# Attention scores of a kernel's last stage: 64-row products with a masked second copy of the keys in place of 32-row products

## The chip, the cores and the metric

The kernel runs on one core of a Trainium2 chip. The metric is the device time of one execution in microseconds (us). TensorE (PE) multiplies matrices into PSUM, VectorE (DVE) and ScalarE (ACT) read PSUM and do element work, GpSimd (POOL) issues indirect transfers and sets memory, and SyncE (SP) issues most of the other transfers. All five run their own instruction streams and wait for each other through semaphores.

## The reference

Eight blocks follow each other over 8 x 256 tokens of 128 features, each as `x = layernorm(x + block(x))`: a recurrent scan, a dense mixture of experts, a latent attention, a second mixture of experts, a gated linear attention, a routed mixture of 160 experts, six layers of linear attention, and last `_L3_ffn_ref`, which is the one that is changed here:

```python
def _L3_ffn_ref(x, router_prob, norm_w, norm_b, q_w, q_b, k_w, k_b, v_w, v_b, o_w, o_b):
    B, T, D, E, H = (4, 256, 128, 4, 8)
    ...
    for e in range(e_cnt):                       # four segments of 64 tokens
        xn = _layernorm(x[:, e * n:(e + 1) * n, :], norm_w, norm_b)
        m = d // 2 ** e                          # 128, 64, 32, 16 features
        xm = xn[..., :m]
        qs.append(jnp.einsum('bnm,dm->bnd', xm, q_w[:, :m]) + q_b)
        ks_.append(jnp.einsum('bnm,dm->bnd', xm, k_w[:, :m]) + k_b)
        vs.append(jnp.einsum('bnm,dm->bnd', xm, v_w[:, :m]) + v_b)
    ...
    attn = jnp.einsum('bhqd,bhkd->bhqk', q, k) * scale      # 8 heads of 16 features
    attn = jax.nn.softmax(attn, axis=-1)
    attn_out = jnp.einsum('bhqk,bhkd->bhqd', attn, v)
    ...
```

So there are 8 heads of 16 features, and the scores of a head are a product over 16 features for 256 queries and 256 keys of each batch element. All data are float32.

## The kernel before

The 2048 tokens are kept as four groups g of 512 tokens (two batch elements of 256 each). Groups 0 and 1 are `first`, groups 2 and 3 are `second`. The two halves go through the blocks shifted against each other, so that a transfer-bound block of one half lies beside a compute-bound block of the other. A scheduler orders each engine's instructions when the kernel is built, by its own estimate of when each would be ready; on the chip every engine runs its stream strictly in that order, so an instruction that waits holds up what stands behind it. Pools give tiles their place in SBUF; a tile that lands where an older one lay waits for the older one's last user.

The routed experts (`place`, `routed_experts`, `gather`) of a half work like this: `place` on GpSimd scatters the tokens' rows to DRAM with 64 indirect transfers (L622), with small memsets (L541) between them as pauses; `routed_experts` loads blocks of rows (`xb<-placed`, L702) and of weights on SP's queue, transposes them (L136, tile ps_m) and multiplies (L729, L740); `gather` reads the results back with 64 indirect transfers (L751) that L757 sums up on DVE. `plan(second)` needs the end of the gated linear attention (L1044 to L1070), the router (L845) and counts (L553 to L560) of the second half, and starts GpSimd's second scatter.

The last part of the program is, in order: the six layers of linear attention of the first half (`layers`, L1110 to L1180; started beside the second half's routed experts), the last block of the first half (`l3_ffn`, whose `run` begins at L1227) beside the six layers of the second half, and the last block of the second half alone.

`l3_ffn` loads its weights on SP's queue (L63, L69, L1222), and GpSimd sets its value tiles (`vs`, L1214), its row maxima (`mx`, L1216) and `ob` (L1220). Then for each group: the tokens are normalized and transposed (L1244, L1246); queries and keys are made by L1254 for the head sets r = 0 and 1 and copied out of PSUM by ACT with a bias (L1255). A head set has four heads, each on a strip of 32 partitions: 16 features, one row that carries the row's maximum, and zeros. So q and k are [128 partitions, r, 512 tokens]. The scores of four heads are four products over 32 rows each, at partitions 0, 32, 64 and 96, into four PSUM banks. TensorE takes such a product as two records in the profile.

`maxima(b, i)` multiplies 128 queries with all 256 keys (L1280, two head sets in a bank) and DVE takes the maximum of every row (L1282). `shifted(b)` transposes the maxima and adds them to the queries' extra row (L1288), which meets the ones in the keys' extra row. `values(b, r)` multiplies 128 keys with all 256 queries (L1298, two key tiles in a bank), and ACT takes the exponentials (L1301). `summed` multiplies with the values (L1309), and `divided` transposes back and divides (L1319, L1321). The output product is L1357. The scores of a batch element are thus made twice, with 32 products of L1280 and 32 of L1298 for a group, so 128 of each in all. Score banks come from two PSUM pools of two banks each, which transposes and other products use as well.

Of the kernel before, what the change touches and what calls it, by code (L numbers as in the profile page):

```python
# [10 lines left out]
F32 = mybir.dt.float32  # L11
I32 = mybir.dt.int32
U32 = mybir.dt.uint32
AF = mybir.ActivationFunctionType
ALU = mybir.AluOpType
AX = mybir.AxisListType

P = 128
# [3 lines left out]
GT = NT // NG  # L22
# [20 lines left out]
def tile_post_ln_blocks(ctx: ExitStack, tc: tile.TileContext, I, out: bass.AP):  # L43
    nc = tc.nc
    V, S, G, PE = nc.vector, nc.scalar, nc.gpsimd, nc.tensor
# [8 lines left out]
    def bank(pool):  # L54
        return pool.tile([P, 512], F32, tag=pool.name, name=pool.name)

    def quarters(t):
        return t.rearrange("p (a b) -> p a b", b=P)

    def load(pool, key, tag=None, by=None):  # L60
        ap = I[key]
        t = pool.tile(list(ap.shape), F32, tag=tag or key, name=tag or key)
        (by or nc.sync).dma_start(out=t, in_=ap)  # L63
        return t
# [1138 lines left out]
    def l3_ffn(es):  # L1203
# [1 line left out]
        width = [D >> e for e in range(4)]  # L1205
        sc = D**-0.5
        wp = es.enter_context(tc.tile_pool(name="f3w", bufs=1))
        wq, wkk, wv, wo, nw, nb, qb, kb, first = (
            load(wp, "F3_" + k) for k in ("q", "k", "v", "o", "norm_w", "norm_b", "qb", "kb", "first")
        )  # L1210
        vb = load_row(wp, "F3_vb")
        for ln in lanes[:2]:
# [14 lines left out]
        def run(ln, g, banks):  # L1227
# [4 lines left out]
            def score():  # L1232
                turn[0] += 1
                return bank(banks[turn[0] % len(banks)])
# [3 lines left out]
            nT = wk.tile([P, GT], F32, tag="nT", name="nT")  # L1238
            nT = nT.rearrange("p (b e c) -> p b e c", b=2, e=4)
            pt = transpose4(zn, ln.ps).rearrange("p (b j) (s c) -> p b (j s) c", b=2, s=2)  # L1240
            for e in range(4):
                scale, bias = nw[:, e : e + 1], nb[:, e : e + 1]
# [4 lines left out]


            qk = wk.tile([P, 2, 2, GT], F32, tag="hT", name="qk")
            q, k = qk[:, 0], qk[:, 1]  # L1250
            for w, bias, t in ((wq, qb, q), (wkk, kb, k)):
                for r in range(2):
                    ps = score()
                    PE.matmul(ps, lhsT=w[:, r, :], rhs=nT.rearrange("p b e c -> p (b e c)"), start=True, stop=True)  # L1254
                    S.activation(t[:, r, :], ps, AF.Identity, bias=bias[:, r : r + 1])  # L1255
            pv = quarters(bank(ln.ps))
            for j in range(4):
                t = 2 * (j % 2)
                PE.matmul(
                    pv[:, j, :], lhsT=nT[:, j // 2, t : t + 2, :].rearrange("p e c -> p (e c)"), rhs=wv,  # L1260
                    start=True, stop=True,
# [6 lines left out]

            at = wk.tile([P, 4, D], F32, tag="qs", name="at")

            strips = [slice(32 * j, 32 * j + 32) for j in range(4)]
            oT = [None]

            def maxima(b, i):
                bs, c = slice(b * T, (b + 1) * T), b * T + i * P
                mx = ln.maxima[:, b]
                ps = [score().rearrange("p (r c) -> p r c", r=2) for _ in strips]
                for r in range(2):
                    for j, hp in enumerate(strips):
                        PE.matmul(ps[j][:, r, :], lhsT=q[hp, r, c : c + P], rhs=k[hp, r, bs], start=True, stop=True)  # L1280
                for j in range(4):
                    V.tensor_reduce(mx[:, i, :, j, DH], ps[j], AX.X, ALU.max, negate=True)  # L1282

# [7 lines left out]
            def values(b, r):  # L1291
                bs = slice(b * T, (b + 1) * T)
                exps = []
                ps = [score().rearrange("p (t c) -> p t c", t=2) for _ in strips]
                for t in range(2):
                    c = b * T + t * P
                    for j, hp in enumerate(strips):
                        PE.matmul(ps[j][:, t, :], lhsT=k[hp, r, c : c + P], rhs=q[hp, r, bs], start=True, stop=True)  # L1298
                for j in range(4):
                    ex = wk.tile([P, 2, T], F32, tag=("vs", "ks", "qT", "y2")[j], name="ex")  # L1300
                    S.activation(ex, ps[j], AF.Exp, scale=sc)  # L1301
                    exps.append(ex)
                return exps
# [11 lines left out]
            def divided(b):  # L1315
# [4 lines left out]
                for r in range(2):  # L1320
# [3 lines left out]
                    )  # L1324

            maxima(0, 0)
            maxima(0, 1)
            shifted(0)
            for r in range(2):
                exps = values(0, r)  # L1330
                maxima(1, r)
                summed(0, r, exps)
            divided(0)
            shifted(1)
            for r in range(2):
                summed(1, r, values(1, r))
# [29 lines left out]
    first, second = (0, 1), (2, 3)  # L1366
# [12 lines left out]
    with ExitStack() as moe:  # L1379
# [72 lines left out]
        gathers(second)  # L1452
    lanes += [Lane(tc, ctx, i) for i in (2, 3)]
    last = l3_ffn(ctx)
    run()
    for g in first:
# [6 lines left out]
def _layout(d):  # L1463

    a = {k: np.asarray(v) for k, v in d.items()}
    f = np.float32
    o = {"x": a["L0_attn_tokens"].reshape(NT, D)}
# [61 lines left out]
    w, d = a["L2_ffn_w_gate"].transpose(0, 2, 1), a["L2_ffn_w_down"].transpose(0, 2, 1)  # L1529
# [29 lines left out]
    def spread(w):  # L1559

        z = np.zeros(w.shape[:-1] + (2, 4, 32), w.dtype)
        z[..., :16] = w.reshape(w.shape[:-1] + (2, 4, 16))
        return z.reshape(w.shape[:-1] + (2, P))

    for k in "qk":
        o["F3_" + k] = spread(a[f"L3_ffn_{k}_w"].T)
        o[f"F3_{k}b"] = spread(a[f"L3_ffn_{k}_b"]).T.copy()
    o["F3_kb"][16::32] = 1.0
    o["F3_v"], o["F3_o"] = a["L3_ffn_v_w"].T, a["L3_ffn_o_w"].T
    o["F3_vb"], o["F3_ob"] = (a[f"L3_ffn_{k}_b"].reshape(1, D) for k in "vo")  # L1570
    o["F3_first"] = (lat[:, None] < (D >> np.arange(4))[None]).astype(f)
# [23 lines left out]
```

## Time and profile before

| what | us |
|---|---|
| median of 3 runs | 1978.19 (1975.71 to 1980.26) |
| profiled execution: its own time | 1984.49 |
| profiled execution: span from first to last instruction | 1982.6 |
| PE busy | 1726.8 (87%) |
| DVE busy | 1200.1 (61%) |
| ACT busy | 889.9 (45%) |
| POOL busy | 385.3 (19%) |
| mean granted TensorE clock | 0.919 |
| L1280, 128 products, records' busy time | 40.6 |
| L1298, 128 products, records' busy time | 44.9 |
| L1282, 64 maxima on DVE | 41.0 (0.682 each) |
| L1301, 64 exponentials on ACT | 34.9 (0.595 each at this shape) |

The profile is one execution. A line of its timeline gives the start in us, the duration, the engine, the line of the program, the operation, the tile written and those read, the shapes, and in brackets how long the engine idled before and what ended that wait. Matmuls of different strips overlap, so the busy time of TensorE is the time in which at least one is under way. A line of the windows view gives a stretch, its length, the busy time (and number of instructions) of PE, PEld (weight loads), DVE, ACT and POOL, then the granted TensorE clock as a share of full speed, the share of the DMA engines and GB/s. In the page's slices each digit is a fortieth of the span: the busy share, or the granted clock, in tenths.

### The profile page before, as it was taken

Reading aid. Unit: us, or ns where it says so; the run is one execution under the profiler, and the core shown is the slowest. Engines: PE = TensorE matmul, PEld = TensorE weight load, DVE = VectorE, ACT = ScalarE, POOL = GpSimd, SP = SyncE. Lnnn points to the kernel's source line nnn. Section 1 sums busy time; section 2 is a strip of 40 time slices with the busy share of each in tenths; the row PEclk is TensorE's granted clock in tenths of the full one; section 3 lists DMA queues with packets and bytes.
Section 4 is the critical chain, followed back from the end, with each engine's and each line's share of the span. In section 5 each row is a group of like instructions: output and inputs, shape, how many; then the busy total and the mean of one; then the engine's idle time right before and its main releaser. Section 6 shows DMA issues by size and latency. Waiting matters only on the chain. (4 is left out here: it accounts for less than half of the span.)

```text
span 1982.6 us, 38359 instructions
## 1 busy us (share of the span) xinstructions
PE 1726.8 (87%) x13996; PEld 1139.8 (57%) x13996; DVE 1200.1 (61%) x3912; ACT 889.9 (45%) x1992; POOL 385.3 (19%) x849
## 2 busy tenths in 40 slices
PE   8999889976999999999779674688877999998887
PEld 6888744544554446644467553466655776665554
DVE  4000255877878656799468811565677887575553
ACT  4555443824765345642424210244444665545433
POOL 1000000000000000007870587850287000000000
PEclk9999989978999999999789766899989999999887
DMA  3000079601434542336218765876011000000000
GB/s 101 3 4 3 3 208 276 178 10 50 116 101 109 157 131 76 102 103 181 58 42 252 249 211 183 262 243 192 22 40 37 1 1 1 1 6 6 1 1 11
DMA packets 161484, 184.97 MB, mean 93 GB/s; under 512 B 20336, under 2 KB 118640, under 8 KB 161296
## 3 DMA queue, kind: packets, MB, share of 16 engines
q1 hardware_dynamic: 143264, 149.47, 26.6%
q0 software_dynamic: 8192, 16.79, 2.9%
q10 hardware_dynamic: 9840, 16.26, 2.2%
q8 instruction: 111, 1.82, 0.4%
q14 instruction: 77, 0.63, 0.1%
HBM read 143.29 MB, written 56.16 MB: 101 GB/s over the span
## 5 line engine op out<-in xcount | busy, mean ns | idle before, releaser
L622 POOL DMA_INDIRECT placed<-x,pl x128 | 127.5, 996 | 990.2 <-DMA wu<-in_F_wu_dram 892.9
L434 ACT ACTIVATE h<-ps_m 128x512 f32<-128x512 f32 x196 | 116.0, 597 | 232.5 <-PE ps_m L432 210.7
L427 PE MATMUL ps_o<-h,wd 128*128 128x512 f32 x384 | 199.0, 603 | 6.4 <-DVE h L440 6.4
L432 PE MATMUL ps_m<-xT,wg 128*128 128x512 f32 x384 | 198.3, 599 | 3.8 <-ACT h L434 3.7
L360 PE MATMUL ps_s<-st,L_a 128*64 128x32 f32 x4096 | 193.2, 222 | 1.1
L360 PEld LDWEIGHTS ps_s<-st,L_a 128*64 128x64 f32 x4096 | 160.5, 136 | 30.0 <-ACT st L369 12.3
L440 DVE TENSOR_TENSOR h<-h,bc 128x512 f32<-128x512 f32 x192 | 131.2, 685 | 49.4 <-ACT h L434 41.9
L369 ACT ACTIVATE st<-ps_s 128x64 f32<-128x64 f32 x512 | 114.8, 224 | 102.3 <-PE ps_s L360 71.1
L751 POOL DMA_INDIRECT got<-made,pl x128 | 122.6, 958 | 135.1 <-DVE cx L1149 105.6
L437 PE MATMUL ps_m<-xT,wu 128*128 128x512 f32 x256 | 134.1, 606 | 6.2 <-ACT h L434 3.5
L541 POOL MEMSET idle<- 128x112 f32 (+1 forms) x576 | 124.8, 217 | 18.5
L427 PEld LDWEIGHTS ps_o<-h,wd 128*128 128x128 f32 x384 | 72.6, 193 | 96.0 <-issue 66.5
L740 PE MATMUL ps_o<-w,xg 64*64 64x128 f32 x1152 | 95.3, 315 | 32.0 <-DVE xg L735 16.4
L432 PEld LDWEIGHTS ps_m<-xT,wg 128*128 128x128 f32 x384 | 71.0, 191 | 86.0 <-issue 65.0
L438 DVE TENSOR_TENSOR h<-h,ps_m 128x512 f32<-128x512 f32 x132 | 89.8, 680 | 45.6 <-PE ps_m L437 40.0
L317 DVE SCALAR_TENSOR_TENSOR outsT<-xnT,L_skip,ps 128x64 f32<-128x64 f32 x32 | 10.4, 324 | 168.3 <-PE ps L305 168.3
L1169 PE MATMUL ps<-nT,A_w 128*128 128x512 f32 x192 | 97.7, 618 | 12.6 <-DVE hT L1171 7.8
L740 PEld LDWEIGHTS ps_o<-w,xg 64*64 64x64 f32 x1152 | 74.7, 155 | 49.2 <-DVE xg L735 20.7
L1175 PE MATMUL ps<-A_w,hT 128*128 128x128 f32 x768 | 98.6, 278 | 4.9 <-DVE hT L1171 3.9
L742 ACT COPY ob<-ps_o 128x512 f32<-128x512 f32 x72 | 42.1, 585 | 133.5 <-PE ps_o L740 99.2
L1175 PEld LDWEIGHTS ps<-A_w,hT 128*128 128x128 f32 x768 | 91.8, 192 | 12.7 <-DVE hT L1171 6.7
L729 PE MATMUL ps_m<-xg,w 128*64 128x64 f32 x1152 | 76.4, 257 | 24.8 <-DMA w<-in_F_w_dram 10.6
(370 smaller groups left out, 3496.7 us busy)
## 6 DMA issues: line engine op xcount, KB each, us to landing
bc<-comb SPq DMA_DIRECT2D x128, 256.0 KB
w<-in_F_w_dram SPq DMA_DIRECT2D x256, 96.0 KB
placed<-zero SPq DMA_DIRECT2D x72, 256.0 KB
xb<-placed SPq DMA_DIRECT2D x72, 256.0 KB
made<-ob ACTq DMA_DIRECT2D x72, 256.0 KB
w<-in_F_wg_dram SPq DMA_DIRECT2D x40, 256.0 KB
w<-in_F_wd_dram SPq DMA_DIRECT2D x40, 256.0 KB
bc<-comb SPq DMA_DIRECT2D x16, 512.0 KB
```

Of the source, the lines that this page charges most:

```text
L360: in_turn(PE.matmul(now[h][sides[c], n % HB // 2, n % 2, s].rearrange("p e f b -> p (e f b)"), lhsT=a_sb[:, n % 2, 4 * h + k, :], rhs=prev ...
L369: made_by = S.activation(st[:, t * 128 : t * 128 + 128].rearrange("p (k e z b) -> p k e z b", k=4, e=2, z=2)[:, :, :, 1], now[h][:, n % HB ...
L427: PE.matmul(acc[g], lhsT=w, rhs=h, start=begin, stop=end, skip_group_check=True)
L432: PE.matmul(pg, lhsT=wg, rhs=xT[g], start=True, stop=True)
L434: gate = S.activation(h, pg, func).ins
L437: PE.matmul(pu, lhsT=wu, rhs=xT[g], start=True, stop=True)
L440: V.tensor_tensor(h, h, bc[:, i * GT : (i + 1) * GT], ALU.mult)
L541: after, last = G.memset(idle[:, :columns], 0.0).ins, after
L622: i = G.indirect_dma_start(placed[h][:, :], bass.IndirectOffsetOnAxis(rw[:, j, c : c + 1], 0), x[g][:, j, :], None).ins
L740: PE.matmul(po[k, i // 2, :], lhsT=h[k, i // 2, :], rhs=wd[i], start=True, stop=True)
L751: i = G.indirect_dma_start(got[:, c, :], None, made[g // 2][:, :], bass.IndirectOffsetOnAxis(row[g][:, j, c : c + 1], 0)).ins
L1175: PE.matmul(po[:, j, :], lhsT=hT[:, f, j * P : (j + 1) * P], rhs=w2[:, f, :], start=(f == 0), stop=(f == 3),)
```

## The change

The keys are kept twice, as `k[0]` and `k[1]`. `k[0]` has the even strips' keys (heads 0 and 2 of a set) and zeros on the odd strips; `k[1]` has the odd strips' keys and zeros on the even ones. ACT makes the first with a scale of one or zero by partition (`strip[:, 0:1]`), and DVE makes the second from the same bank with `tensor_scalar`. A score product then runs over the 64 rows of a pair of strips, with the queries of both heads and the keys of one: the other head's rows add zeros. The products of strips 0 and 1 are on the upper 64 rows of the array, those of 2 and 3 on the lower 64, and the source asks for them in the order 0, 2, 1, 3. The number of products, their columns, their banks, the maxima and the exponentials stay. `k[1]` gets two tiles of 4 KB a partition in the stage's weight pool `wp`, the mask `F3_strip` is one more small load, and the bias of the keys `F3_kb` has two masked sets of columns.

```diff
--- before.py
+++ after.py
@@ -1205,8 +1205,8 @@
         width = [D >> e for e in range(4)]
         sc = D**-0.5
         wp = es.enter_context(tc.tile_pool(name="f3w", bufs=1))
-        wq, wkk, wv, wo, nw, nb, qb, kb, first = (
-            load(wp, "F3_" + k) for k in ("q", "k", "v", "o", "norm_w", "norm_b", "qb", "kb", "first")
+        wq, wkk, wv, wo, nw, nb, qb, kb, first, strip = (
+            load(wp, "F3_" + k) for k in ("q", "k", "v", "o", "norm_w", "norm_b", "qb", "kb", "first", "strip")
         )
         vb = load_row(wp, "F3_vb")
         for ln in lanes[:2]:
@@ -1247,12 +1247,17 @@
 
 
             qk = wk.tile([P, 2, 2, GT], F32, tag="hT", name="qk")
-            q, k = qk[:, 0], qk[:, 1]
-            for w, bias, t in ((wq, qb, q), (wkk, kb, k)):
-                for r in range(2):
-                    ps = score()
-                    PE.matmul(ps, lhsT=w[:, r, :], rhs=nT.rearrange("p b e c -> p (b e c)"), start=True, stop=True)
-                    S.activation(t[:, r, :], ps, AF.Identity, bias=bias[:, r : r + 1])
+            q = qk[:, 0]
+            k = qk[:, 1], wp.tile([P, 2, GT], F32, tag=f"k{g % 2}", name="k")
+            for r in range(2):
+                ps = score()
+                PE.matmul(ps, lhsT=wq[:, r, :], rhs=nT.rearrange("p b e c -> p (b e c)"), start=True, stop=True)
+                S.activation(q[:, r, :], ps, AF.Identity, bias=qb[:, r : r + 1])
+            for r in range(2):
+                ps = score()
+                PE.matmul(ps, lhsT=wkk[:, r, :], rhs=nT.rearrange("p b e c -> p (b e c)"), start=True, stop=True)
+                S.activation(k[0][:, r, :], ps, AF.Identity, bias=kb[:, 0, r : r + 1], scale=strip[:, 0:1])
+                V.tensor_scalar(k[1][:, r, :], ps, strip[:, 1:2], kb[:, 1, r : r + 1], ALU.mult, ALU.add)
             pv = quarters(bank(ln.ps))
             for j in range(4):
                 t = 2 * (j % 2)
@@ -1268,7 +1273,7 @@
 
             at = wk.tile([P, 4, D], F32, tag="qs", name="at")
 
-            strips = [slice(32 * j, 32 * j + 32) for j in range(4)]
+            strips = [(j, j % 2, slice(64 * (j // 2), 64 * (j // 2) + 64)) for j in (0, 2, 1, 3)]
             oT = [None]
 
             def maxima(b, i):
@@ -1276,8 +1281,8 @@
                 mx = ln.maxima[:, b]
                 ps = [score().rearrange("p (r c) -> p r c", r=2) for _ in strips]
                 for r in range(2):
-                    for j, hp in enumerate(strips):
-                        PE.matmul(ps[j][:, r, :], lhsT=q[hp, r, c : c + P], rhs=k[hp, r, bs], start=True, stop=True)
+                    for j, o, hp in strips:
+                        PE.matmul(ps[j][:, r, :], lhsT=q[hp, r, c : c + P], rhs=k[o][hp, r, bs], start=True, stop=True)
                 for j in range(4):
                     V.tensor_reduce(mx[:, i, :, j, DH], ps[j], AX.X, ALU.max, negate=True)
 
@@ -1294,8 +1299,8 @@
                 ps = [score().rearrange("p (t c) -> p t c", t=2) for _ in strips]
                 for t in range(2):
                     c = b * T + t * P
-                    for j, hp in enumerate(strips):
-                        PE.matmul(ps[j][:, t, :], lhsT=k[hp, r, c : c + P], rhs=q[hp, r, bs], start=True, stop=True)
+                    for j, o, hp in strips:
+                        PE.matmul(ps[j][:, t, :], lhsT=k[o][hp, r, c : c + P], rhs=q[hp, r, bs], start=True, stop=True)
                 for j in range(4):
                     ex = wk.tile([P, 2, T], F32, tag=("vs", "ks", "qT", "y2")[j], name="ex")
                     S.activation(ex, ps[j], AF.Exp, scale=sc)
@@ -1566,6 +1571,8 @@
         o["F3_" + k] = spread(a[f"L3_ffn_{k}_w"].T)
         o[f"F3_{k}b"] = spread(a[f"L3_ffn_{k}_b"]).T.copy()
     o["F3_kb"][16::32] = 1.0
+    o["F3_strip"] = (np.arange(P)[:, None] // 32 % 2 == np.arange(2)[None]).astype(f)
+    o["F3_kb"] = np.where(o["F3_strip"][:, :, None] > 0, o["F3_kb"][:, None, :], f(0.0))
     o["F3_v"], o["F3_o"] = a["L3_ffn_v_w"].T, a["L3_ffn_o_w"].T
     o["F3_vb"], o["F3_ob"] = (a[f"L3_ffn_{k}_b"].reshape(1, D) for k in "vo")
     o["F3_first"] = (lat[:, None] < (D >> np.arange(4))[None]).astype(f)
```

## The prediction

> **What bounds the kernel now.** I read the page's slices first, then the windows of the last stage, then the timelines of TensorE and GpSimd.
>
> ```profile
> span 1982.6 us, 38359 instructions
> ...
> PE   8999889976999999999779674688877999998887
> ...
> PEclk9999989978999999999789766899989999999887
> ```
>
> TensorE is the busiest engine up to the end, and its granted clock sags in the last slices, where L1280 and L1298 run. In stretches (us, then busy time of PE, PEld, DVE, ACT, POOL, then the granted clock):
>
> ```profile
> 1646.00:1805.00 159.00, 151.96 (x934) 101.89 (x932) 100.29 (x305) 82.93 (x191) 0.00 (x0) 0.97 0.01 3
> 1868.00:1983.00 115.00, 92.92 (x544) 54.69 (x544) 51.48 (x161) 41.70 (x92) 0.00 (x0) 0.77 0.02 5
> 1906.10:1909.50 3.40, 3.40 (x9) 2.12 (x8) 1.10 (x2) 0.77 (x2) 0.00 (x0) 0.50 0.00 0
> 1930.00:1933.40 3.40, 3.04 (x20) 1.68 (x16) 0.76 (x2) 2.06 (x4) 0.00 (x0) 1.00 0.00 0
> 1933.40:1936.80 3.40, 3.40 (x20) 1.85 (x23) 0.00 (x0) 1.35 (x3) 0.00 (x0) 0.51 0.00 0
> ```
>
> The first half's L1206 stage (1646 to 1805, beside the second half's layers) is TensorE's: 152.0 of 159.0 us busy. The second half's (1868 to the end) has it busy for 92.9 of 115 us at a mean clock of 0.77. The third row stays at half clock though TensorE is busy throughout; the fourth is busy for 3.04 us, and yet the clock falls right after it (fifth row). So busy time is not what the gate follows here. The trace's clock changes only at multiples of 3.41 us. I cut it so, and summed for each window the streaming time of its matmuls (columns by 1.2 per ns, half that at half clock) times the share of the 128 rows that they use. The clock fell after windows with a share of 0.38 or less (39 falls; the lowest of 446 windows that kept full clock is 0.38) and came back after 0.70 or more (38 rises; the 55 that stayed at half reach 0.76). The fourth row's window by hand: two runs of two score matmuls on 32 rows give 2 x 0.85 x 32/128 = 0.43 us, the rest 0.63, together 1.06 of 3.41, a share of 0.31.
>
> What a score costs, from TensorE's timeline (x counts records, two for each matmul):
>
> ```profile
> 1761.69 1.17 PE L1280 MATMUL ps<-qk 32*128 32x256 f32 x16
> ...
> 1930.82 1.13 PE L1298 MATMUL ps<-qk 32*128 32x256 f32 x4 [0.36 <-ACT ex L1301]
> ...
> 1941.07 2.11 PE L1280 MATMUL ps<-qk 32*128 32x256 f32 x16
> ...
> 1049.02 1.09 PE L740 MATMUL ps_o<-w,xg 64*64 64x128 f32 x16
> ```
>
> Eight matmuls over four strips of 32 rows take as long as two on one strip: about 1.08 us from their start to the next instruction's, two rounds of 0.427 and some 0.21 of turnover; at half clock it is double (2.11). The last row has 64-row products of 128 columns: eight in 1.09 us, four rounds of 0.213 and the turnover, so two 64-row tiles do run side by side.
>
> The other place is far from the diff's lines:
>
> ```profile
> 965.16 0.96 POOL L622 DMA_INDIRECT placed<-x,pl  x1 [0.16 <-issue]
> 966.12 0.26 POOL L541 MEMSET idle<- 128x176 f32 x1
> 966.31 0.96 POOL L1214 MEMSET vs<- 128x1024 f32 x1
> ...
> 970.75 0.96 POOL L622 DMA_INDIRECT placed<-x,pl  x1 [0.17 <-issue]
> ```
>
> ```profile
> 1039.59 1.12 PE L136 MATMUL ps_m<-ident,xb 128*128 128x128 f32 x4 [10.00 <-DMA xb<-placed]
> ```
>
> Five memsets of this stage (L1214, L1216, L1220) stand among GpSimd's scatters. The scatter after them starts 5.59 us after the one before instead of the usual 1.99, and when the scatters end (1035.4) all engines but the DMA are waiting: TensorE idles 10.0 us for the first rows of the routed experts.
>
> **The change, part by part.**
>
> *Moved memsets and loads: -3.6.* The pool of this stage grows by two key buffers (8 KB a partition) and lands elsewhere in memory. In the changed program's order the five memsets stand behind GpSimd's last gather, and the 14 loads (now 15, with F3_strip) are the last on SP's queue but for the four stores of the output; they wait for the last sum of L757, at 1530.8 in this trace. They issue at 0.33 to 0.60 us each, so are done by about 1545; the first user, L1353, ran at 1637. That cover of 90 us makes them free, and only the stores stand behind them. The scatters gain 5.59 - 1.99 = 3.60 us, and the start at 1039.6 comes that much earlier. Against it: 15 of l2_attn's matmuls (13 of L1052 to L1054 at 0.22 us, one L1044, one L1045) now stand behind the wait for these rows, and one block of L740 and one of L136 no longer stand ahead of the last L560: some 2.0 us more of TensorE before plan(second), which starts GpSimd's next scatters (1109). Bounds: -5.6 (shorter queues as well) to +4 (the new order costs as much again). I take -3.6: the routed blocks on SP and TensorE start from the earlier rows.
>
> *Fewer strips side by side, first half: +6.0.* By the order in which each program issues its score matmuls, cut into runs between other matmuls, a run's rounds are those of its fullest strip (00112233 as much as 01230123 took 1.08 to 1.10 us in the trace: strips don't wait for each other). First half: 63 rounds in 33 runs become 81 in 31. That is 18 x 0.427 - 2 x 0.21 = 7.3 us; with TensorE busy 95.6% nearly all of it counts; I take 6.0, since its 7 us of idle time can take some. Bounds 3 to 7.7.
>
> *Second half: +5.5.* 54 rounds in 24 runs become 74 in 16: 20 x 0.427 - 8 x 0.21 = 6.8 us, by the busy share 0.81: 5.5. Bounds 2 to 10 (some of it at half clock).
>
> The Trainium skill (TensorE: Matmul & The Clock Gate, Part 3, Packing small matmuls) says of matmuls: "strict FIFO, no reordering". By that, 00112233 is five rounds and the counts are 77 to 90 and 74 to 82, so 21 rounds more instead of 38; the trace, with 1.09 us for it, disagrees.
>
> *The clock: -11.* With 64 rows a lone score stream counts 0.5 instead of 0.25, two count 1. Four stretches at half clock hold score work. (B) 1933.4 to 1943.7, 10.2 us, fully busy: the window ahead goes from 0.31 to (1.06 + 0.43)/3.41 = 0.44 and no longer drops the clock: 5.1 us less TensorE time, of which I take 4.2, since exps (L1301) run in it too. (C) 1960.8 to 1971.0: the window ahead, at 0.20, comes to about 0.41, on the edge: half of 5, 2.5. (A) 1899.3 to 1916.4: it starts with TensorE idle, which stays; the clock should be back one or two windows earlier (each 1.7 us saved): 2.5. (D) 1680.9 to 1691.1: one window, 1.7. Sum 10.9. Bounds: nothing, to 47.8 us of stretches halved and by their busy share of 0.92, 22; but an idle start remains in A and D, so I use 17.
>
> The same page (Part 1, The HAM clock gate) lets busy time release the clock and idle windows throttle it. By it nothing is gained here; the windows above, busy and at half clock, speak against it.
>
> *Second copy of the keys: +1.0.* Eight DVE tensor_scalar of 128x512 out of PSUM; no such row exists, the nearest (tensor_tensor L1264 of that size) takes 0.69 us: 5.5 us. They run beside ACT's copy of the same bank, on an engine busy 63% and 45% of the two stages. ACT's own copy gains a scale from memory: L1095, with scale and bias, takes 0.777 against 0.687 of L1255, 8 x 0.09 = 0.7 us. Behind the DVE's come the vs sum (L1264) and the maxima, which wait for the scores anyway. Bounds 0 and 6.2; I take 1.0.
>
> **Sum.** -3.6 + 6.0 + 5.5 - 11 + 1.0 = -2.1 us. The profiled execution took 1984.5 us (span 1982.6), 6.3 above the median of 1978.19 (1975.7 to 1980.3); I take the difference off the median: 1976.
>
> **Rivals.**
> - *The gate counts only busy time, or zeros count as idle rows*: the clock term is nil, and the sum is +8.9: 1987, slower. Against: the windows above, and that nearly half of the rows of each 32-row strip are zeros already and count in my shares in full. It decides if fewer than about 6 us come back from the clock. 0.17.
> - *Rounds are hidden, clock comes back whole*: the second half waits for exps and maxima (22 us of TensorE idle), 20 rounds vanish in it, A and C recover fully (-16): -3.6 + 6 + 1.5 - 16 + 1 = -11: 1967. For: at full clock its TensorE work is well below its span. 0.20.
> - *The new order of the routed stage costs time*: the +4 end instead of -3.6, rest as summed: +5.5: 1984. For: TensorE, DVE and DMA are all near full from 1050 to 1100, so 2 us late there may delay GpSimd's 104 us of scatters. 0.16.
> - *Strips in order* (the FIFO rule): 17 rounds fewer added, some 6 us: 1970. 0.05.
> - *The change does not do what it says*: the program shows 64-row tiles throughout and the order 0, 2, 1, 3 only in part (runs such as 0000); in the parts where only one half streams nothing is side by side. It is in the counts.
>
> **How the numbers follow.** The forecast, about no change, has 0.42, with its own range 1970 to 1982 (0.11 of it faster, 0.22 same, 0.09 slower). About 0.2% (4 us) can be told from no change here, so same is 1974.2 to 1982.1. Faster: 0.11 + 0.20 + 0.05 = 0.36; same: 0.22 + 0.02 (rival three's mild end) = 0.24; slower: 0.09 + 0.17 + 0.14 = 0.40. The range takes in the second rival's 1967 and most of the first's: 1966 to 1988.
>
> **What would show it.** The first L136 of xb some 3.6 us earlier; runs of eight score records in 64-row tiles at about 1.9 us instead of 1.08; the mean clock from 1868 on at 0.85 or more, with no fall while scores stream; the first half's stage 5 to 7 us longer, the second's 3 to 6 shorter. A clock that stays near 0.77, or a first half not longer, would prove the steps wrong.

## The result and the profile after

| what | before | after |
|---|---|---|
| median, us (20 runs each) | 1982.72 | 1976.28 |
| ratio after / before | 1 | 0.9968 [0.9953, 0.9983] |
| profiled execution: its own time, span | 1984.49, 1982.6 | 1971.65, 1969.9 |
| first L136 of `xb` | 1039.6 | 1036.5 |
| first gather of the routed experts, L751 | 1213.4 | 1218.1 |
| last L740 ends | 1422.4 | 1421.9 |
| last sum of L757 starts | 1530.8 | 1529.2 |
| from there to the last L1175 | 365.1 | 361.7 |
| last L1175 to the end (second half's last block alone) | 86.8 | 78.9 |
| mean granted clock | 0.919 | 0.929 |

The kernel is 0.32% faster, 6.4 us between medians. The same program, run again below as e10_after_again, was 0.61% faster than before, 11.1 us, so its gain is known as 0.3 to 0.6%. The two spans differ by 12.7 us because the profiled execution of before took 1.8 us more than its median and that of after 4.6 us less; a single profile is therefore read for where time lies, and the ratio for how much. In the changed kernel the lines behind L1254 have moved by four or five: L1258 makes the keys, L1259 and L1260 copy them, L1285 and L1303 are the two score products. One execution each of the changed kernel, e2_scores, e7_rows32_old and e9_issue took 2072 to 2082 us at a lower clock and is left out of the ratios; in e2_scores it was the profiled one, so that kernel was run again as e8_scores_again.

The page's slices of the changed kernel (span, TensorE's busy tenths, granted clock):

```profile
span 1969.9 us, 38416 instructions
...
PE   8999889976999999999879775579977899999787
...
PEclk9999989978999999999787967799989999999889
```

The last three clock digits are 8, 8, 9 where they were 8, 8, 7. By windows, the two stretches of the last stage that the prediction showed (the second from 1868 to the end, as there):

```profile
1646.00:1805.00 159.00, 153.73 (x955) 106.19 (x953) 108.78 (x334) 84.55 (x199) 0.00 (x0) 0.99 0.01 4
1868.00:1970.00 102.00, 81.03 (x530) 54.58 (x528) 52.39 (x154) 40.44 (x89) 0.00 (x0) 0.89 0.02 6
```

The clock of the second is 0.89 where before had 0.77. TensorE's timeline shows what a score costs now:

```profile
1036.51 1.12 PE L136 MATMUL ps_m<-ident,xb 128*128 128x128 f32 x4 [8.25 <-DMA xb<-placed]
...
1902.67 1.14 PE L1285 MATMUL ps<-qk 64*128 64x256 f32 x8
1903.64 1.13 PE L1285 MATMUL ps<-k,qk 64*128 64x256 f32 x8
```

The last two rows are one run of eight products (16 records) on 64-row tiles: four rounds. The seven such runs of the first half, at full clock, take 1.93 to 2.04 us to the next other matmul, against 1.08 for eight products on 32 rows; the one shown starts 0.2 us behind a stretch at half clock and takes 2.23. And on GpSimd, before and then after:

```profile
1034.44 0.96 POOL L622 DMA_INDIRECT placed<-x,pl  x1 [0.16 <-issue]
...
1109.16 0.98 POOL L622 DMA_INDIRECT placed<-x,pl  x1 [72.90 <-DVE pl L618]
```

```profile
1031.49 0.96 POOL L622 DMA_INDIRECT placed<-x,pl  x1 [0.16 <-issue]
...
1113.94 0.97 POOL L622 DMA_INDIRECT placed<-x,pl  x1 [80.63 <-DMA xb<-placed]
```

The first row of each is the last scatter of the first half, 2.9 us earlier after the change; the second is the first scatter of the second half, 4.8 us later. The profile names a load of xb as what ended the last wait, but in both kernels the plan's first L618 ends just ahead of that scatter, at 1108.89 and 1113.66, 0.27 and 0.28 us before it (before, then after):

```profile
1108.72 0.17 DVE L618 TENSOR_TENSOR pl<-pl,pl 128x32 uint32<-128x32 uint32 x1
```

```profile
1113.49 0.17 DVE L618 TENSOR_TENSOR pl<-pl,pl 128x32 uint32<-128x32 uint32 x1
```

### The profile page after: what moved, and what is told of

Same layout as the page of the kernel before. It is cut to its first block, busy times and chain, and to the rows that moved or that the text cites. A ratio compares the mean times of both kernels' runs of the same rounds, so it can differ in the third digit from the quotient of the medians.

```text
span 1969.9 us, 38416 instructions
## 1 busy us (share of the span) xinstructions
PE 1720.3 (87%) x13996; PEld 1146.1 (58%) x13996; DVE 1204.4 (61%) x3920; ACT 890.6 (45%) x1992; POOL 385.8 (20%) x849
## 5 line engine op out<-in xcount | busy, mean ns | idle before, releaser
L440 DVE TENSOR_TENSOR h<-h,bc 128x512 f32<-128x512 f32 x192 | 131.2, 686 | 48.8 <-ACT h L434 41.8
L369 ACT ACTIVATE st<-ps_s 128x64 f32<-128x64 f32 x512 | 114.7, 224 | 101.9 <-PE ps_s L360 70.7
L751 POOL DMA_INDIRECT got<-made,pl x128 | 122.7, 958 | 128.7 <-DMA made<-ob 102.1
L740 PE MATMUL ps_o<-w,xg 64*64 64x128 f32 x1152 | 93.5, 310 | 34.6 <-DVE xg L735 34.0
L740 PEld LDWEIGHTS ps_o<-w,xg 64*64 64x64 f32 x1152 | 73.3, 153 | 51.0 <-DVE xg L735 41.2
L1175 PE MATMUL ps<-A_w,hT 128*128 128x128 f32 x768 | 97.6, 278 | 4.9 <-DVE hT L1171 4.8
L1175 PEld LDWEIGHTS ps<-A_w,hT 128*128 128x128 f32 x768 | 91.7, 192 | 12.4 <-DVE hT L1171 7.0
```

What stands on the lines that cost most here:

```text
L440: V.tensor_tensor(h, h, bc[:, i * GT : (i + 1) * GT], ALU.mult)
L740: PE.matmul(po[k, i // 2, :], lhsT=h[k, i // 2, :], rhs=wd[i], start=True, stop=True)
L751: i = G.indirect_dma_start(got[:, c, :], None, made[g // 2][:, :], bass.IndirectOffsetOnAxis(row[g][:, j, c : c + 1], 0)).ins
L1175: PE.matmul(po[:, j, :], lhsT=hT[:, f, j * P : (j + 1) * P], rhs=w2[:, f, :], start=(f == 0), stop=(f == 3),)
```

## The experiments

All kernels of one job share the runs of the kernel before. The table of all kernels comes first, because each is read against the others. "Routed" runs from the first L136 of `xb` to the end of the last L740, "tail" from the start of the last L757 to the end. "Scores" is the part of the tail from the first score matmul of every run to the next other matmul, summed; "rest" is the rest of the tail. "Half" is the time at half clock behind 1540 (the clock's record runs some 2 us past the last instruction). "Old" is the placement of memsets and loads of the kernel before, "moved" that of the changed kernel.

| kernel | rows, placement | median, us | ratio | routed | tail | scores | rest | half |
|---|---|---|---|---|---|---|---|---|
| before | 32, old | 1982.7 to 1987.0 | 1 | 382.8 | 451.8 | 85.2 | 366.7 | 71.6 |
| after | 64, moved | 1976.28 | 0.9968 [0.9953, 0.9983] | 385.4 | 440.6 | 85.2 | 355.4 | 42.0 |
| e1_placement | 32, moved | 1975.21 | 0.9952 [0.9928, 0.9976] | 385.9 | 442.4 | 75.0 | 367.3 | 62.6 |
| e2_scores, e8_scores_again | 64, old | 1963.67, 1964.47 | 0.9890 [0.9856, 0.9924], 0.9871 [0.9834, 0.9908] | 377.9 | 433.2 | 85.6 | 347.6 | 17.6 |
| e4_half | 32 then 64, moved | 1984.09 | 0.9993 [0.9967, 1.0019] | 386.5 | 448.6 | 88.0 | 360.6 | 52.5 |
| e5_small | 64, moved | 1976.75 | 0.9951 [0.9926, 0.9976] | 386.4 | 443.0 | 85.2 | 357.7 | 48.8 |
| e6_rows32 | 32, moved | 1980.94 | 0.9952 [0.9926, 0.9978] | 391.8 | 438.8 | 76.4 | 362.4 | 64.3 |
| e7_rows32_old | 32, old | 1971.30 | 0.9904 [0.9871, 0.9937] | 379.8 | 440.0 | 76.3 | 363.8 | 61.2 |
| e9_issue | 32, old | 1976.91 | 0.9936 [0.9913, 0.9959] | 380.1 | 450.9 | 77.5 | 373.4 | 81.6 |
| e10_after_again | 64, moved | 1974.63 | 0.9939 [0.9914, 0.9964] | 384.9 | 441.2 | 85.2 | 356.0 | 45.4 |
| e11_rows32_again | 32, moved | 1971.94 | 0.9935 [0.9911, 0.9958] | 383.5 | 444.3 | 79.2 | 365.1 | 74.6 |
| e12_issue3210 | 32, old | 1971.48 | 0.9952 [0.9926, 0.9978] | 378.2 | 442.4 | 80.4 | 362.0 | 68.8 |
| e13_issue1302 | 32, old | 1968.00 | 0.9917 [0.9886, 0.9948] | 375.5 | 440.3 | 73.4 | 367.0 | 70.7 |

In the row of e2_scores the profile is that of e8_scores_again. Medians are compared within a job only: e1, e2, e4 and e5 were one (before 1984.51), e6 to e9 the second (1987.01), e10 to e13 the third (1985.73).

### e1_placement: the placement without the scores

The kernel before with the two key buffers reserved and not used:

```diff
             q, k = qk[:, 0], qk[:, 1]
+            wp.tile([P, 2, GT], F32, tag=f"k{g % 2}", name="k")
```

> The kernel before with 32-row scores, and two tiles of 4 KB reserved in the stage's pool and used by nothing, so that the five memsets and the weight loads of this stage move to the end of their queues as in the changed kernel. Theory (the gain of the tail is the clock's, through the rows): the first L136 of xb near 1036.5 as in the changed kernel, at most 1 to 3 us of gain by the end of L757, then a tail (from the last L757 to the end) of 448 to 455 us as before, with half clock in the last stage while scores stream; total 0 to 4 us under before. Rival (the gain is the placement's and its new order's): tail about 441 us and total 5 to 10 us under before.

Ratio 0.9952: with no product of 64 rows and no second copy, the kernel gains as much as the whole change. The rival was met. But the gain does not come from where the memsets were: the routed part took 385.9 us, 3.1 more than in the profile of before, and the tail 9.4 less. Nor did half clock stay in the last stage. From the last L1175 to the end the clock is 0.85 where before has 0.74 (its line stands with e12 below), with 32 rows as before:

```profile
1898.10:1974.00 75.90, 62.70 (x468) 38.11 (x466) 40.32 (x116) 30.02 (x66) 0.00 (x0) 0.85 0.03 8
```

### e2_scores and e8_scores_again: the scores without the placement

The changed kernel with the second copy in two tiles that the stage already has:

```diff
-            k = qk[:, 1], wp.tile([P, 2, GT], F32, tag=f"k{g % 2}", name="k")
+            odd = [wk.tile([P, GT], F32, tag=t, name="k") for t in ("zn", "y1")]
+            k = [qk[:, 1, 0], qk[:, 1, 1]], odd
...
-                        PE.matmul(ps[j][:, r, :], lhsT=q[hp, r, c : c + P], rhs=k[o][hp, r, bs], start=True, stop=True)
+                        PE.matmul(ps[j][:, r, :], lhsT=q[hp, r, c : c + P], rhs=k[o][r][hp, bs], start=True, stop=True)
```

> The 64-row scores with the second copy of the keys in tiles that are free at that time (those of zn and xb), so that the stage's pool, memsets and loads stay where they were before. Theory: the first L136 of xb near 1039.6 as before, the tail about 441 us (438 to 445), the clock at full while scores stream, total 4 to 9 us under before. Rival (placement): tail about 452 us, total as before.

> The version with 64 rows and the old placement once more, for a profile of an undisturbed execution. Theory (rows and clock): the ratio is again 0.986 to 0.992; the tail from the last layer norm of line 757 to the end is 437 to 441 us against 451.8 before, half clock after 1540 is 35 to 50 us, and the routed stage ahead of it takes its 382 to 383 us, so that the gain lies in the tail alone. Rival (the order of the routed stage): the routed stage takes 375 us as in the disturbed profile, and the tail is no shorter than the changed kernel's 440.7.

1.1% and 1.3% faster than before, some 21 us where 4 to 9 were expected, and the fastest of all: it beats both kernels (1963.67 against 1976.75 of e5_small, whose order of instructions is the changed kernel's, in the same job). Of the second expectation each side had a part: the tail is 7 to 8 us shorter than the changed kernel's (433.2, and 17.6 us at half clock, both better than expected), and the routed part, 377.9, is 4.9 us shorter than in the profile of before. The two kernels' orders are the same up to the last stage but for one small load, so that this is no more than executions of one order differ by: the routed part took 375.5 to 382.8 us in the six profiles of the old placement.

### e4_half: 32 rows in the first half, 64 in the second

```diff
+                if g < 2:
+                    S.activation(k[0][:, r, :], ps, AF.Identity, bias=kb[:, 2, r : r + 1])
+                    continue
...
+            if g < 2:
+                strips = [(j, 0, slice(32 * j, 32 * j + 32)) for j in range(4)]
```

> The changed kernel with 32-row scores (one copy of the keys) for the first half and 64-row scores for the second. The prediction's step (the first half loses about 6 us by 64 rows): from the last L757 to the last L1175 356 to 360 us against 361.4 of the changed kernel, and the total 3 to 6 us under the changed kernel. Rival (the first half gains too, because half clock goes there as well): 363 to 367 us to the last L1175, and the total 2 to 5 us over the changed kernel. The last stage of the second half is 78 to 81 us in both (from the last L1175 to the end, 79.2 in the changed kernel).

No gain: 1984.09 against before's 1984.51. Taking the 64 rows out of the first half, where the prediction let them cost 6 us, makes the kernel no faster than e5_small beside it (1976.75); its tail is 448.6 us. The rival's range was met up to the last L1175 (363.2 us), but the comparison is not clean. The last stage of the second half, whose edit is that of the changed kernel, took 85.4 us where 78 to 81 was expected: its order changed too. And 64 rows cost the first half's score runs nothing: they take 41.5 us here with 32 rows, 8.0 of them at half clock, and 41.4 in the changed kernel, none at half clock.

### e5_small: the other head's keys not quite zero

```diff
-    o["F3_strip"] = (np.arange(P)[:, None] // 32 % 2 == np.arange(2)[None]).astype(f)
+    o["F3_strip"] = np.where(np.arange(P)[:, None] // 32 % 2 == np.arange(2)[None], f(1.0), f(1e-3))
```

> The changed kernel with the other head's keys of a pair scaled by 0.001 instead of 0 (so the scores have a small part of the other head's in them); every instruction is the same. Theory (the gate counts rows by instruction): granted clock and time as in the changed kernel, within 3 us. Rival (zeros count as idle rows, or draw less): the clock in the last stage moves by more than 0.03 from 0.91.

The clock is 0.927 against 0.929, the time at half clock 48.8 us against 42.0 and 45.4 in the two profiles of the changed kernel, the ratio 0.9951. Zeros or a thousandth of the other head's keys in the masked rows: the clock does not tell them apart. Keys of full size were not tried.

### e6_rows32 and e7_rows32_old, e10_after_again and e11_rows32_again: 64 rows against 32

The strongest test of the rows: two copies of the keys as in the changed kernel, only the products cut back to 32 rows, once at each placement. SyncE's and GpSimd's orders are those of the 64-row counterpart, the others' differ inside the last stage only.

```diff
-            strips = [(j, j % 2, slice(64 * (j // 2), 64 * (j // 2) + 64)) for j in (0, 2, 1, 3)]
+            strips = [(j, j % 2, slice(32 * j, 32 * j + 32)) for j in (0, 2, 1, 3)]
```

> The changed kernel with its two copies of the keys and its placement, but the score products cut to 32 rows again, in the issue order 0, 2, 1, 3. The orders of the transfers and of GpSimd are those of the changed kernel; TensorE's, VectorE's and ScalarE's differ from it only inside the last stage. Theory (rows and clock): 110 rounds in place of 135 save about 25 x 0.21 = 5 us, and the half clock returns to the tail by some 20 to 30 us (49 us or less of half clock after 1540 in the changed kernel, 72 in the kernel before), so that the time is 2 to 8 us above the changed kernel's, near 1980 to 1986 where the kernel before reads 1984. Rival (placement and its order alone): the time is the changed kernel's within 3 us, about 1975 to 1978, as it was for the placement alone; half clock after 1540 about 50 to 63 us.

> The same edit on the version that keeps the old placement: two copies of the keys, 32 rows, issue order 0, 2, 1, 3. Theory (rows and clock): without the 64 rows the gain of that version (ratio 0.989) is gone, the ratio against the kernel before is 0.997 to 1.003 and half clock after 1540 is 60 to 75 us. Rival (the order that the scheduler finds for the last stage): the ratio stays at 0.987 to 0.992, although no product has 64 rows.

> The changed kernel beside its 32-row counterpart on one chip, with the same runs of the kernel before. Theory (64 rows raise the clock, 32 rows save rounds): the two effects nearly cancel at this placement, ratio 0.994 to 0.998 against the kernel before and within 0.2% of the 32-row counterpart. Rival (64 rows are worth some 0.3% as at the old placement): 4 us or more faster than the counterpart.

> The changed kernel with 32-row products in the order 0, 2, 1, 3, once more. Theory: ratio 0.994 to 0.998, within 0.2% of the changed kernel run beside it. Rival: 4 us or more slower than the changed kernel, as the 32-row version at the old placement was 6.8 us slower than its 64-row counterpart.

The expectation of e6 counts 135 rounds in the changed kernel; by its order of issue they are 81 + 74 = 155, as in the prediction, so 45 rounds were at stake and not 25.

At the moved placement e10 and e11, on one chip, give 0.9939 and 0.9935: the rows are worth nothing that can be told. At the old one e8 took 1964.47 us and e7 1971.30 (1959.5 to 1969.8 and 1969.6 to 1975.2): the rows are worth some 7 us. That rests on six executions of each: the intervals of the two ratios overlap, and the ratio of e2, the same program as e8, would make it 3 us. Both e6 and e7 keep most of the gain without any 64-row product, against the first theory. Of that theory the clock's part held: 64.3 and 74.6 us at half clock with 32 rows, 42.0 and 45.4 with 64 at the moved placement, 61.2 and 17.6 at the old.

The stretch from the last L1175 to the end, by windows, for e7_rows32_old and then e8_scores_again:

```profile
1889.00:1967.80 78.80, 63.64 (x428) 37.87 (x426) 37.08 (x111) 29.99 (x66) 0.00 (x0) 0.80 0.03 8
```

```profile
1886.70:1958.80 72.10, 59.03 (x428) 39.19 (x426) 37.09 (x111) 29.48 (x66) 0.00 (x0) 0.94 0.03 8
```

The same number of matmuls, TensorE busy for the same share (63.64 / 78.80 = 0.81, 59.03 / 72.10 = 0.82), and a clock of 0.80 against 0.94. The order of the last stage differs between the two as well, and e1 shows that an order moves the clock by 0.1; but in this stretch every profile with 32 rows has 0.74 to 0.85 and every one with 64 rows 0.88 to 0.94, so the rows raise it. For the whole tail the table gives the price: scores +9.3 us (more rounds), rest -16.2 (faster clock in the main: in the rest half clock falls from 44.3 to 13.0 us, worth at most 15.7). At the moved placement, as means of two profiles each: scores 85.2 against 77.8, +7.4; rest 355.7 against 363.8, -8.1.

### e9_issue, e12_issue3210, e13_issue1302: another order of issue, nothing else

The kernel before, with 32 rows and one copy; only the order in which the four strips are asked for changes. Up to the last stage every engine's order is that of before. For e9:

```diff
-            strips = [slice(32 * j, 32 * j + 32) for j in range(4)]
+            strips = [(j, slice(32 * j, 32 * j + 32)) for j in (0, 2, 1, 3)]
...
-                    for j, hp in enumerate(strips):
+                    for j, hp in strips:
```

and 3, 2, 1, 0 and 1, 3, 0, 2 for the other two.

> The kernel before with one copy of the keys and 32 rows, with only the order in which the four strips of a product are issued changed from 0, 1, 2, 3 to 0, 2, 1, 3. All strips still run side by side; rounds are 106 in place of 117 by the new order of records. Theory (rows and clock): within 0.3% of the kernel before, ratio 0.997 to 1.003, half clock after 1540 60 to 75 us. Rival (any new order of the last stage moves the time by as much as the change did): the ratio is off 1 by 0.4% or more, either way.

> The kernel before, 32 rows and one copy of the keys, with the strips issued 3, 2, 1, 0: the same work, and an order of the last stage that nobody aimed at. GpSimd's and the transfers' orders are those before. Theory (the kernel before happens to have a costly order in its last stage): like the order 0, 2, 1, 3 it is faster than before, ratio 0.991 to 0.997. Rival (the gain of 0, 2, 1, 3 was its own): ratio 0.998 to 1.003.

> The kernel before with the strips issued 1, 3, 0, 2: by the build order 91 rounds of score products in place of 117 before, 106 for 0, 2, 1, 3 and 100 for 3, 2, 1, 0. Theory (rounds are on the path that sets the end): 26 x 0.21 to 0.43 = 5 to 11 us less than before, ratio 0.9945 to 0.997, and the order of times follows the rounds: below 3, 2, 1, 0, which is below 0, 2, 1, 3. Rival (rounds are hidden or given back by a lower clock, and the order of the rest decides): no such order of times; half clock after 1540 above 72 us as for 0, 2, 1, 3 (82).

All three are faster, 0.64%, 0.48% and 0.83%, with intervals that end below 1: the order in which the kernel before issues its last stage is a costly one, and an order that was aimed at nothing gains as much as the change. Since nothing ahead of the last stage differs, the gain must lie in it, though e9's one profile, 3 us above its median, does not show it (tail 450.9). The differences to before's median of the same job, 10.1, 14.3 and 17.7 us, follow the rounds (117 before, then 106, 100 and 91); the ratios do not (0.9936, 0.9952, 0.9917), so that rounds are the cause is likely and not shown. e13 gained more than expected of it: 26 rounds x 0.427 and 14 runs x 0.21 are 14.0 us at full clock, and 34.4 of the last 80.1 us are at half clock; its score runs took 11.8 us less than before's.

Windows of the stretch from the last L1175 on, before and then e12_issue3210:

```profile
1895.90:1982.60 86.70, 69.44 (x426) 40.16 (x424) 34.90 (x107) 30.00 (x66) 0.00 (x0) 0.74 0.02 7
```

```profile
1887.50:1968.30 80.80, 63.26 (x426) 37.17 (x424) 34.99 (x107) 29.89 (x66) 0.00 (x0) 0.74 0.02 7
```

The same 426 matmuls and the same clock, but TensorE is busy for 6.2 us less, and the stretch is 5.9 shorter: with 46 rounds in place of 54 in the second half, more of the products lie side by side, without a change of the clock. Of the 5.9 us, 3.9 lie in the score runs (43.1 us in this stretch before, 39.2 here); the other 2 were not traced to a line.

## Why the prediction was right, and where it was not

The time was forecast as 1976.0 and measured as 1976.28. That the figure agrees is luck. The sum was -2.1 us, no change that can be told; the change brought -6.4, and -11.1 when it was run again. The sum was taken off the median of three runs, 1978.19, and the median of twenty is 4.5 us higher. Two steps failed, the term of the moved memsets and the longer first half, and a term was missing, the new order.

*The prediction's own signs.* The first L136 came 3.1 us earlier (3.6 was said), eight products take 1.93 us or more (1.9), and the clock from 1868 on is 0.89 (0.85 or more). But the first half's stage should have become 5 to 7 us longer, and "a first half not longer" was to prove the steps wrong. It became 7.2 us shorter, from the first query product to the last output products (before, then after; the other profile of the changed kernel, e10, agrees):

```profile
1648.98 1.12 PE L1254 MATMUL ps<-nT,F_q 128*128 128x512 f32 x2 [0.24 <-DVE nT L1244]
...
1806.76 0.68 PE L1357 MATMUL ps<-F_o,aT 128*128 128x128 f32 x4 [0.22 <-DVE xb L1360]
```

```profile
1646.33 1.02 PE L1254 MATMUL ps<-nT,F_q 128*128 128x512 f32 x2
...
1796.87 0.61 PE L1362 MATMUL ps<-F_o,aT 128*128 128x128 f32 x4
```

That is 157.8 and 150.5 us. The score runs in it did grow, from 38.8 to 41.4 us; the rest of the stage shrank by more. So the step that the rounds of the first half lengthen it by 6 us did not hold.

*Moved memsets and loads, -3.6: the wrong sign.* The gap between the scatters went and the first rows come earlier, but only by 3.1 us in this profile and 1.9 as a mean (1037.1 in seven profiles of the moved placement, 1039.0 in six of the old). Then the new order of the routed stage takes it back and more: the first gather starts at 1218.0 against 1212.9 and the last L757 at 1531.3 against 1526.7 (means of the same profiles; for the gather and for the routed part's length, 386.3 against 379.1, the two groups do not overlap). So the term is about +4.6, with a standard error of 1.5. (The loads were free, as forecast: they issue from 1529.6 to 1537.3, over 100 us ahead of the first query product.) The step that failed is "I take -3.6": its other end, +4, the third rival's, was right, and so was its place. The plan of the second half comes later, as the last matmuls of L560 do (1086.5 before, 1092.0 after), and with it GpSimd's second scatter, as the two rows above show.

*Rounds, +6.0 and +5.5.* Right in direction, too small in the sum. In the first half of the changed kernel, where no score run meets half clock, 81 rounds in 31 runs should take 81 x 0.427 + 31 x 0.21 = 41.1 us, and its runs sum to 41.4. But the count by the fullest strip is not always enough: a run of 22 products in its second half, 12 rounds, took 5.92 us at full clock in place of 5.33, and before's first half took 38.8 us for 33.8, only 2.1 of it from half clock. With half-clock time counted by half, and without TensorE's waits inside the runs, the score runs of the tail come to 66.6 us before and 81.4 after. That is +14.8 (4.7 in the first half, 10.1 in the second), more than the 11.5 of the two terms. Yet as they stand they took no longer than before, 85.2 and 85.2: 27.3 us of before's score runs were at half clock and 3.9 of after's, worth 11.7 us, and the waits inside them fell from 4.9 to 1.8 us.

*The clock, -11.* Right in direction, and of about the right size. In the tail 71.6 us at half clock became 42.0; these 29.6 us are worth at most half of that, 14.8. Of that 11.7 is in the score runs, so only some 3 us are left for the rest, and the -11.3 of the rest (366.7 to 355.4) is in the main not the clock's. Beside the 32-row counterparts the 64 rows bring half clock from 69.4 to 43.7 us as means, worth at most 12.9, which the added rounds take back. That the clock would not fall at all while scores stream was a little too much: from 1885, where the second half's scores begin, it falls once among them, at 1895.7, and a run of eight products takes 3.71 us there; from 1902.5 to 1960.5 it is full. Nor is 0.85 from 1868 on a sign of the rows alone: e1, with 32 rows, has 0.86.

The count of array rows in use holds again: in the trace of after the clock falls behind windows with a share of 0.38 or less, and the lowest that keeps full clock is 0.37. It speaks against busy time, as the pair e7 and e8 does by itself. The Trainium skill (TensorE: Matmul & The Clock Gate, Part 1, The HAM clock gate) has the gate set by how busy the array has recently been; here the busy share is the same and the clock is not, so the rule needs the rows.

*Second copy, +1.0.* Its premise was wrong: DVE's copy does not run beside ACT's. The changed kernel's instructions of L1260, with what ended the idle time before them:

```profile
L1260 DVE TENSOR_SCALAR k<-ps,F_strip,F_kb x8: 805/810/811, 1649.3 to 1909.5; 128x512 f32<-128x512 f32 x8
its engine sat idle before it (us, times) until:
  ACT qk L1259: 4.7, 4
```

0.810 us each, not 0.69, and four of the eight wait for ACT, 4.7 us in all. In all eight DVE starts 0.03 to 0.34 us after ACT has ended on that bank. What this costs at the end was not measured apart. The Trainium skill (PSUM — Partial Sum Buffer, PSUM bank collisions raise a hardware error) says that two engines must not access the same partitions of one bank at the same time, reads included; in this program they never do. A step that lets ACT and DVE read the same bank side by side should have been checked against it.

*What the sum lacked: the order.* Rows against rows, the sum's +11.5 - 11 = +0.5 was right: e10 against e11 measures nothing. The tail's -11.2 us is then +14.8 for the rounds, at most -14.8 for the clock, -3.1 for waits inside the score runs, and at least -8 elsewhere. A gain of the tail (451.8 to 440.6) is there as well with 32 rows (438.8 and 444.3). It comes with the new order that the scheduler makes of the last stage once anything in it changes, and before's order is a bad one among those tried. For the order of issue alone this is shown (e9, e12, e13). For e1_placement, e6 and e11 it follows only by exclusion, since their counts of rounds (111 and 110 against 117) give 4 us of the 10 or so that the tail gains. In e1 the new order also moves the clock: half clock in the last stage falls from 45.8 to 23.2 us, though over the tail only by some 9, worth at most 4.5. What is left stays open.

*The rivals.* The first (busy time, zeros idle) falls by e5 and by e7 beside e8. The second (rounds hidden, clock whole) puts the tail at 6 + 1.5 - 16 + 1 = -7.5 us, nearer to the measured -11.2 than the sum's +1.5, for a reason that is only half its own: the rounds were not hidden, the clock paid for them. The third (the routed stage) happened, at its price, beside the gain of the order, so the time did not come out slower. The fourth (strips in order) gives 90 rounds in the first half, 44.9 us, and 41.4 were measured; in the second half's long runs neither count is right (the 22 products above would be 14 rounds, 6.19 us, by the strict order). The fifth (the change doesn't do what it says) does not hold: 64-row tiles run two side by side.

## What to carry to other kernels

A change inside a stage that a scheduler orders is two changes: what was edited, and a new order. Give the order a term and measure it: make the same edit without its supposed benefit (here: the same copies and the same issue order with 32 rows), and one that only shuffles equal instructions. When a change gets a buffer of its own, try it in buffers that the stage already has: the placement here cost 4.6 us elsewhere, and beside it the rows were worth nothing. Why they are worth some 7 us in one order of the last stage and nothing in the other is not shown. The version with the 64 rows and the old placement was 1.1 to 1.3% faster than before.

## What was not expected of the hardware

The granted clock answered to rows that multiply nothing but zeros as to rows that carry data (0.929 with zeros, 0.927 with small keys). In kernels whose streams are the same up to the last stage (before, e9, e12, e13) the last L757 came at 1530.8, 1527.1, 1525.9 and 1522.7: one profile beside another says nothing about less than some 8 us there, and the stage tables above had to be read in groups.
